# Two edge layers of a graph network: six steps for a group of edges in place of three, results of the matrix engine read one group later, more buffers for gathered rows, and a gate split into pieces

## The chip, the cores and the metric

The kernel runs on one core of one Trainium2 chip. A core has five engines that run side by side, each with its own queue of instructions: TensorE (PE in the profile; its weight loads have a row of their own, PEld), VectorE (DVE), ScalarE (ACT), GpSimd (POOL) and SyncE (SP), which issues most of the plain transfers. Engines wait for each other through semaphores. The metric is the device time of one execution in microseconds, the median over runs.

## The reference

There are 3125 nodes with 256 features each and 53125 edges, given in the order of their destination node. Four layers follow each other; each adds its result to `x` and starts from a layer norm of `x`.

```python
x = x + L0_gnn(layernorm(x), edge_index, edge_weight, ...)
x = x + L0_ffn(layernorm(x), ...)      # mixture of 16 experts, two for each node
x = x + L1_gnn(layernorm(x), ..., src, dst, edge_type)
x = x + L1_ffn(layernorm(x), ...)      # half of the nodes, chosen by a router
```

The first graph layer (layer 0) sums over the edges of a source node, with four heads:

```python
score = a_s[:, src] + a_d[:, dst] + aw_e * elem + ab
w = exp(-relu(score / 20.0))
out = segment_sum(w * feats[dst], src) / segment_sum(w, src)
```

The second (layer 1) sums over the edges of a destination node, with 200 types of relation:

```python
score = h[src] @ w_src + h[dst] @ w_dst + rel_emb[etype] @ w_rel
alpha = exp(leaky_relu(score)); alpha = alpha / alpha
agg = segment_sum((h[src] + rel_emb[etype]) @ weight_neighbor * alpha, dst)
x = x + relu(agg) + where(in_deg > 0, h @ loop_weight, h @ evolve_loop_weight)
```

The router of the last layer takes one weight for each node, `z @ wr + br`, and the 1561 nodes with the largest weights go through a feed-forward layer with weights `w1` (256 x 1024) and `w2` (1024 x 256).

## The kernel before

Edges are sorted by the block of 128 nodes that they are summed into. There are 25 blocks; each of the first 24 has room for 18 tiles of 128 edges, the last for 8. A tile is one edge for each of the 128 partitions. Six tiles make a group (`GRP`), so 24 blocks have three groups each and the last has one of six tiles and one of two: 74 groups and 440 tiles in a layer. Both graph layers run the same loop (`pipelined`, L966) over the stages that `edge_stages` (L874) returns, with their own `messages` and `finish`.

In a step of the loop each stage works on another group: `gather` on group g, `message` on g - 1, `add` on g - 2.

- `gather` fetches the far nodes' rows from a table in HBM, one indirect transfer by POOL for each tile (L907), into `rows`, of which there are `deep` buffers: five in layer 0, four in layer 1. It makes on DVE the one-hot `oh` of each edge's place in the block (L915), and from a transfer that repeats the edges' places over all partitions (`wide`, L897, on SP) the transposed masks `hot` (L924; three for a group in layer 1, one in layer 0).
- `message` multiplies the masks on TensorE with the near nodes' scores (L933), reads the sum from PSUM on DVE (`near`, L940), and calls `messages`. In layer 0 that is three small DVE steps, two exponentials on ACT and the scaling of the rows on DVE (L1099). In layer 1 it is an add (L1636), the weight with its exponential (L1595 to L1598), a one-hot of the relation written beside the row (L1639), and the one-hot `oh` scaled by each edge's weight on ACT into a second tile, `ohw` (L1645).
- `add` multiplies one-hots with rows on TensorE and sums a block in PSUM (L953). After a block's last group DVE reads the sum (`acc`, L961) and `finish` runs.

In layer 0, `finish` divides by the sum of weights and adds to `x`, and `done` of `gate` (L1185) runs for the tiles that are complete: after tiles 5, 10, 15, 20, 23 and 25 it normalizes them, turns them, multiplies them with the gate's weights (L1196), adds the bias (L1200), and after tiles 15, 23 and 25 picks the two experts (`choose`, L1148). In layer 1, `loops` (L1650, called as `early`) multiplies a block's nodes with both loop weights (L1654) into `held_ps`; `finish` (L1660) turns the counts of relations (L1666, L1669), multiplies them with the relations' features (L1672), and adds everything to `x` on DVE (L1679 to L1689).

PSUM is short: `ps_hold` holds constant numbers in its first half (`numbers`, read by L915 and L1639) and in its second half `held_ps` (the exponentials in layer 0, loop products in layer 1); `ps_sums` holds two blocks' sums; four buffers of one bank each (`ps_b`) serve all the rest.

After layer 1, `depths` (L1950) runs. `route` (L1732) normalizes the nodes in two batches (tiles 0 to 21, then 22 to 24) and takes their weights for the router on DVE (L1740), and stores them to HBM (ztab, L1746). The square root of its first batch (L167) has a dependency on the layer's last gather. `chosen` finds the 1561 largest, their rows are gathered (L1970), and the feed-forward layer follows (L2016, L2028). Its weights `w1` and `w2` are loaded by `router` (L1706, L1708), ahead of layer 1.

The order of each engine's instructions isn't that of the program. A planner lists them when the kernel is built: earlier lines of the program go first, but what is ready in the planner's own view of time may pass what is not. `keep_in_program_order` ties an instruction behind the one that the program wrote before it for the same engine.

Of the kernel before, what the change touches and what calls it, by code (L numbers as in the profile page):

```python
# [22 lines left out]
class _Kernel:  # L23
# [850 lines left out]
    def edge_stages(  # L874
        self, pool, st, table, width, into, near, others, messages, W, sums, finish, early=None, deep=3
    ):

# [24 lines left out]
        def gather(g, b, k, n, head, last):  # L902
            if head:
                now[b] = [spread(i, b) for i in range(len(st["wide"]))]
            rows = pool.tile([P, G, into], F32, name="rows", bufs=deep)
            for j in range(n):
                self.last_gather = nc.gpsimd.indirect_dma_start(  # L907
                    out=rows[:, j, :width], out_offset=None, in_=table,
                    in_offset=bass.IndirectOffsetOnAxis(
                        ap=st["idx"][:, k + j : k + j + 1], axis=0  # L910
                    ),
                )
            sh = [P, n, P]
            oh = pool.tile([P, G, P], F32, name="oh", bufs=3)
            nc.vector.tensor_tensor(  # L915
                oh[:, :n, :], numbers[:, None, :P].to_broadcast(sh),
                st["row"][:, k : k + n, None].to_broadcast(sh), op=OP.is_equal,
            )
            lo = (k - self.first[b]) // 2
            hots = []  # L920
            for i, (at, _) in enumerate([(self.pcol1, None)] + others):
                w = now[b][min(i, 1)][:, lo : lo + n // 2, : 2 * P]
                t = pool.tile([P, G // 2, 2 * P], BF16, name=f"hot{i}", bufs=2)
                nc.vector.tensor_scalar(t[:, : n // 2, :], w, at, None, op0=OP.is_equal)  # L924
                hots.append(t)
            return rows, oh, hots

        def message(g, b, k, n, head, last, rows, oh, hots):
            pe = self.ps_b("ps_near")
            picks = [near[:, b]] + [v for _, v in others]  # L930
            for j in range(n):
                for i, (t, v) in enumerate(zip(hots, picks)):
# [5 lines left out]
                    )  # L938
            own = pool.tile([P, G, nv], F32, name="near")
            nc.vector.tensor_reduce(  # L940
                own[:, :n, :],
                pe[:, : n * 3 * nv].rearrange("p (j q v) -> p j v q", q=3, v=nv), AX.X, OP.add,
            )
            if early is not None and k - self.first[b] == G:
                early(b)
            return messages(k, n, rows, own, oh)

        def add(g, b, k, n, head, last, oh, msg):
            if head:
                now["sum"] = sums2[:, b % 2 * 512 : (b % 2 + 1) * 512]  # L950
            ps = now["sum"]
            for j in range(n):
                nc.tensor.matmul(  # L953
                    ps[:, :W], oh[:, j, :], msg[:, j, :],
                    start=(head and j == 0), stop=(last and j == n - 1),
                )
            if last:
                more = pool.tile([P, W], F32, name="more")
                nc.sync.dma_start(more, sums[b])
                acc = pool.tile([P, W], F32, name="acc")  # L960
                nc.vector.tensor_add(acc, ps[:, :W], more)  # L961
                finish(b, acc)

        return gather, message, add

    def pipelined(self, stages, fill=()):  # L966
# [4 lines left out]
        for step in range(len(groups) + len(stages) - 1):  # L971
            if step > 2:
                next(fill, None)
            for i, stage in enumerate(stages):
                g = step - i
                if 0 <= g < len(groups):
                    done[g] = stage(g, *groups[g], *(done.pop(g, None) or ()))
# [77 lines left out]
    def heads_edges(self, st, fill, done):  # L1055
# [26 lines left out]
        with self.tc.tile_pool(name="edge0", bufs=2) as pool:  # L1082
# [7 lines left out]
            def messages(k, n, rows, near, oh):  # L1090
# [13 lines left out]
                return oh, rows  # L1104

            def finish(b, acc):
# [7 lines left out]
                done(b)  # L1114

            self.pipelined(self.edge_stages(
                pool, st, self.table0, W, W, near, [], messages, W, self.sums0, finish, deep=5
            ), fill)

    def gate(self, pool):


        nc, a, NT, D = self.nc, self.a, self.NT, self.D
# [59 lines left out]
        def done(b):  # L1185
            if b + 1 not in ends:
                return
            i = ends.index(b + 1)
            t0, t1 = ends[i - 1] if i else 0, b + 1
            self.norm_tiles(xn, t0, t1)  # L1190
            nc.sync.dma_start(xv[:, t0:t1, :], xn[:, t0:t1, :])
            pl = self.ps_b("ps_logit")
# [7 lines left out]
            nc.vector.tensor_tensor(  # L1200
# [3 lines left out]
            )  # L1204
            if t1 in choices:
                choose(choices[choices.index(t1) - 1], t1)

        return done
# [412 lines left out]
    def relations_edges(self, st):  # L1621
# [4 lines left out]
        with self.tc.tile_pool(name="edge1", bufs=2) as pool:  # L1626
# [7 lines left out]
            def messages(k, n, rows, near, oh):  # L1634
# [8 lines left out]
                ow = pool.tile([P, G, P], F32, name="ohw", bufs=3)  # L1643
                for j in range(n):
                    nc.scalar.activation(  # L1645
                        ow[:, j, :], oh[:, j, :], AF.Copy, scale=s[:, 1, j : j + 1]
                    )
                return ow, rows
# [11 lines left out]
            def finish(t, acc):  # L1660
# [10 lines left out]
                for i, (r0, n) in enumerate(rc):  # L1671
# [3 lines left out]
                    )  # L1675
                pw = self.held_ps
                xt = self.x[:, t, :]
                v = pool.tile([P, D], F32, name="agg")
                nc.vector.tensor_add(v, acc[:, :D], pr[:, :D])  # L1679
# [14 lines left out]
                early=loops, deep=4,  # L1694
# [4 lines left out]
    def router(self, pool):  # L1699
# [5 lines left out]
        w1 = pool.tile([P, C, HID], F32, name="w1")  # L1705
        nc.sync.dma_start(w1, a["L1_ffn_w1"].rearrange("(c p) h -> p c h", p=P))  # L1706
        w2 = pool.tile([P, HC, D], F32, name="w2")
        nc.sync.dma_start(w2, a["L1_ffn_w2"].rearrange("(c p) d -> p c d", p=P))  # L1708
# [12 lines left out]
        self.ffn_w = w1, w2, b1, b2  # L1721
# [228 lines left out]
    def depths(self):  # L1950
# [6 lines left out]
        w1, w2, b1, b2 = self.ffn_w  # L1957
        with self.tc.tile_pool(name="whom", bufs=1) as pool:
            for t in range(NT):
                self.route(t)  # L1960
# [197 lines left out]
```

## Time and profile before

| | |
|---|---|
| median of 10 runs | 2010.92 us (2007.0 to 2015.16) |
| the profiled execution | 2009.2 us, of which the span of its instructions is 2007.5 us |
| TensorE busy | 1470.6 us (73%) |
| VectorE busy | 1170.1 us (58%) |
| GpSimd busy | 1124.0 us (56%) |
| ScalarE busy | 423.8 us (21%) |
| gathers of layer 0 | first at 281.97 us, last ends at 836.10 us |
| gathers of layer 1 | first at 1287.37 us, last ends at 1841.57 us |
| weights of the router complete | 1872.6 us |
| first product of the feed-forward layer (L2016) | 1907.6 us |

Between the layers lie the experts (about 883 to 1230 us) and the features of layer 1. A line of the groups gives the source line, the engine, the operation, output<-inputs by the program's names, how often it ran, its busy time with the mean in nanoseconds, and then the idle time of the engine just before it with what ended most of that; "issue" is time in which the engine waited for nothing that the profile shows. A line of the waits gives who waited for whom, the total in microseconds, how many times, and the longest. A line of the timeline gives start, duration, engine and line, and in square brackets the idle time before it. In a table of windows a pair stands for each engine: busy time and, in brackets, instructions.

### The profile page before, as it was taken

The page shows a single profiled execution, that of the slowest core. Times are in us where ns is not written, and L with a number is a line of the kernel's source. Part 1 is how long each engine was busy: PE and PEld are TensorE (multiplying, and loading weights), DVE is VectorE, ACT ScalarE, POOL GpSimd, SP SyncE. Part 2 cuts the span into 40 slices and gives each one's busy share as a digit, 9 for nine tenths or more (in the row PEclk, how much of TensorE's full clock was granted, in tenths as well). Part 3 has the DMA queues.
Part 4 walks back from the last instruction along what each step waited for, and adds up shares of the span by engine and source line. Part 5 has one row for each costly group of instructions (what it writes and reads, how often), then busy time and mean ns, then how long its engine had stood idle before and what let it go on. Part 6 is the DMA issues. An engine that isn't in the chain of part 4 may idle for free. (4 is left out here: it accounts for less than half of the span.)

```text
span 2007.5 us, 22343 instructions
## 1 busy us (share of the span) xinstructions
PE 1470.6 (73%) x6602; PEld 920.6 (46%) x6602; DVE 1170.1 (58%) x3010; ACT 423.8 (21%) x1148; POOL 1124.0 (56%) x1133
## 2 busy tenths in 40 slices
PE   3677705475665666639999996498898888897398
PEld 1155504354444444426666664344444444443266
DVE  8999925575656665653322224467676677665631
ACT  1311100010101001102122223433233233334221
POOL 1058867777777777513333320267777777775051
PEclk8589957777777777759999998789999999998699
DMA  3042134454555555349899995575556655663140
GB/s 112 1 154 77 31 100 132 133 161 135 155 142 151 137 154 143 107 154 340 305 313 317 316 312 173 181 206 171 162 165 177 174 163 162 171 170 96 61 137 17
DMA packets 250714, 324.52 MB, mean 162 GB/s; under 512 B 38128, under 2 KB 185008, under 8 KB 250582
## 3 DMA queue, kind: packets, MB, share of 16 engines
q1 hardware_dynamic: 192214, 179.00, 28.4%
q0 software_dynamic: 51760, 137.35, 24.4%
q10 hardware_dynamic: 6608, 6.62, 1.0%
q8 instruction: 57, 0.93, 0.2%
q14 instruction: 75, 0.61, 0.1%
HBM read 286.26 MB, written 36.61 MB: 161 GB/s over the span
## 5 line engine op out<-in xcount | busy, mean ns | idle before, releaser
L907 POOL DMA_INDIRECT rows<-table,s_idx x880 | 835.6, 950 | 282.3 <-issue 236.1
L953 PE MATMUL ps_sums<-rows,oh 128*128 128x260 f32 x880 | 286.1, 493 | 163.1 <-issue 150.2
L953 PE MATMUL ps_sums<-rows,ohw 128*128 128x457 f32 x880 | 369.2, 561 | 10.1 <-ACT ohw L1645 9.9
L953 PEld LDWEIGHTS ps_sums<-rows,oh 128*128 128x128 f32 x880 | 214.3, 251 | 222.5 <-issue 162.7
L953 PEld LDWEIGHTS ps_sums<-rows,ohw 128*128 128x128 f32 x880 | 163.1, 194 | 167.9 <-issue 120.4
L1387 PE MATMUL ps_h<-w,x_t 128*128 128x512 f32 x448 | 203.9, 597 | 0.0
L924 DVE TENSOR_SCALAR hot<-wide,pcols 128x768 bf16<-128x768 bf16 (+1 forms) x296 | 174.1, 594 | 13.6 <-DMA wide<-s_w 7.5
L1409 POOL DMA_INDIRECT ytab<-y,back x56 | 55.0, 981 | 204.2 <-DVE y L1408 195.3
L1393 DVE TENSOR_TENSOR hid<-hid,ps_h 128x512 f32<-128x512 f32 x56 | 38.5, 688 | 198.7 <-ACT hid L1392 198.7
L915 DVE TENSOR_TENSOR oh<-ps_hold,s_row 128x768 f32<-128x768 f32 (+1 forms) x148 | 139.5, 942 | 20.8 <-PE ps_sums L953 20.8
L1645 ACT ACTIVATE ohw<-oh,s 128x128 f32<-128x128 f32 x440 | 136.4, 388 | 67.5 <-DVE s L1598 56.8
L609 POOL DMA_INDIRECT s_tab<-s_rec,s_to x65 | 124.5, 1916 | 30.4 <-issue 19.4
L1099 DVE TENSOR_TENSOR rows<-rows,ps_hold 128x1536 f32<-128x1536 f32 x74 | 128.3, 1733 | 0.6 <-ACT ps_hold L1097 0.3
L1387 PEld LDWEIGHTS ps_h<-w,x_t 128*128 128x128 f32 x448 | 81.5, 192 | 80.7 <-issue 80.6
L1093 DVE TENSOR_TENSOR s<-near,rows 128x24 f32<-128x24 f32 x74 | 13.6, 183 | 176.7 <-DMA rows<-table,s_idx 164.1
L1639 DVE TENSOR_TENSOR rows<-ps_hold,s_val 128x1200 f32<-128x1200 f32 x74 | 102.9, 1391 | 20.9 <-PE ps_hold L1654 20.8
L933 PEld LDWEIGHTS <-hot 128*128 128x128 bf16 x1760 | 61.6, 99 | 100.8 <-DVE hot L924 64.5
L1404 PE MATMUL ps_y<-w,h_t 128*128 128x256 f32 x448 | 105.9, 379 | 0.7 <-ACT h_t L202 0.7
L1097 ACT ACTIVATE ps_hold<-s 128x24 f32<-128x24 f32 x74 | 14.3, 193 | 434.5 <-DVE s L1095 235.8
L1404 PEld LDWEIGHTS ps_y<-w,h_t 128*128 128x128 f32 x448 | 85.0, 190 | 36.0 <-issue 26.3
L593 DVE TENSOR_TENSOR s_hv<-s_hk,s_dig 128x400 f16<-128x400 f16 x208 | 99.0, 648 | 0.0
L1362 POOL DMA_INDIRECT xg<-xtab,who x56 | 54.0, 964 | 77.5 <-DVE who_w L1337 46.3
(410 smaller groups left out, 2002.5 us busy)
## 6 DMA issues: line engine op xcount, KB each, us to landing
w<-in_L_ffn_w_dram SPq DMA_DIRECT2D x168, 512.0 KB
wide<-s_w SPq DMA_DIRECT2D x72, 576.0 KB
rows<-table,s_idx POOLq DMA_INDIRECT x880
sums<-sums_z SPq DMA_DIRECT2D x5, 1142.5 KB
more<-sums SPq DMA_DIRECT2D x25, 228.5 KB
yg<-ytab SPq DMA_DIRECT2D x5, 1024.0 KB
sums<-sums_z SPq DMA_DIRECT2D x5, 650.0 KB
table<-f ACTq DMA_DIRECT2D x5, 650.0 KB
```

The source lines that it names most:

```text
L593: nc.vector.tensor_tensor(rec[:, i], hk[:, i, :, None, :].to_broadcast(sh), dig[:, None, :, t0 + 2 * i : t0 + 2 * i + 2].to_broadcast(sh), ...
L609: d = nc.gpsimd.indirect_dma_start(out=tab, out_offset=bass.IndirectOffsetOnAxis(ap=to[:, i : i + 1], axis=0), in_=out[:, k * CH * V : (k ...
L907: self.last_gather = nc.gpsimd.indirect_dma_start(out=rows[:, j, :width], out_offset=None, in_=table, in_offset=bass.IndirectOffsetOnAxis( ...
L915: nc.vector.tensor_tensor(oh[:, :n, :], numbers[:, None, :P].to_broadcast(sh), st["row"][:, k : k + n, None].to_broadcast(sh), op=OP.is_equal,
L924: nc.vector.tensor_scalar(t[:, : n // 2, :], w, at, None, op0=OP.is_equal)
L933: nc.tensor.matmul(pe[:, j * 3 * nv : (j + 1) * 3 * nv], t[:, j // 2, j % 2 * P : (j % 2 + 1) * P], v.rearrange("p q v -> p (q v)"), start ...
L953: nc.tensor.matmul(ps[:, :W], oh[:, j, :], msg[:, j, :], start=(head and j == 0), stop=(last and j == n - 1),)
L1099: nc.vector.tensor_tensor(rows[:, :n, :HO].rearrange("p j (h o) -> p j h o", o=O), rows[:, :n, :HO].rearrange("p j (h o) -> p j h o", o=O) ...
L1387: nc.tensor.matmul(ph[:, i * HID : (i + 1) * HID], xt[:, c, :], w12[:, i, c, :], start=(c == 0), stop=(c == C - 1),)
L1404: nc.tensor.matmul(py[:, :D], ht[:, c, :], w3[:, c, :], start=(c == 0), stop=(c == HC - 1))
L1639: nc.vector.tensor_tensor(rows[:, :n, R0:], self.numbers[:, None, :R].to_broadcast(sh), st["val"][:, k : k + n, None].to_broadcast(sh), op ...
L1645: nc.scalar.activation(ow[:, j, :], oh[:, j, :], AF.Copy, scale=s[:, 1, j : j + 1])
```

## The change

The loop has six stages. `gather` keeps the transfers and the masks. `pick` has the products of masks and near scores, and makes `oh`, of which there are now four buffers. `message` reads `near` and calls `messages`. `add` has the products and issues the load of `more`. `finished` calls `early`, reads `acc` and calls `finish`. `closed` calls `close`, a new second part of layer 1's `finish` that begins with `agg`. A group so passes `message` two steps after its gather instead of one, `add` three steps after it instead of two, and its block is read one or two steps later again.

The DVE reads of `near`, `acc`, `agg` and `logits` are tied to program order. `rows` has seven buffers in layer 0 and six in layer 1. In layer 1 ACT scales `oh` in place, and the three buffers of `ohw` go. `done` of the gate is a generator: the norm and the store in one step, the turned tiles and products in the next, the bias and the choice in a third; its products go to the second half of `held_ps` and no longer to a buffer of `ps_b`. `w1` and `w2` are loaded in `depths`, in the pool that is opened after layer 1's.

```diff
-        def gather(g, b, k, n, head, last):
+        def gather(z, b, k, n, head, last):
...
-            sh = [P, n, P]
-            oh = pool.tile([P, G, P], F32, name="oh", bufs=3)
-            nc.vector.tensor_tensor(
-                oh[:, :n, :], numbers[:, None, :P].to_broadcast(sh),
-                st["row"][:, k : k + n, None].to_broadcast(sh), op=OP.is_equal,
-            )
...
-        def message(g, b, k, n, head, last, rows, oh, hots):
-            pe = self.ps_b("ps_near")
+        def pick(z, b, k, n, head, last):
+            z["pe"] = pe = self.ps_b("ps_near")
...
+            sh = [P, n, P]
+            z["oh"] = oh = pool.tile([P, G, P], F32, name="oh", bufs=4)
+            nc.vector.tensor_tensor(
+                oh[:, :n, :], numbers[:, None, :P].to_broadcast(sh),
+                st["row"][:, k : k + n, None].to_broadcast(sh), op=OP.is_equal,
+            )
+
+        def message(z, b, k, n, head, last):
             own = pool.tile([P, G, nv], F32, name="near")
-            nc.vector.tensor_reduce(
+            self.tc.keep_in_program_order(nc.vector.tensor_reduce(
                 own[:, :n, :],
-                pe[:, : n * 3 * nv].rearrange("p (j q v) -> p j v q", q=3, v=nv), AX.X, OP.add,
-            )
+                z["pe"][:, : n * 3 * nv].rearrange("p (j q v) -> p j v q", q=3, v=nv),
+                AX.X, OP.add,
+            ))
+            messages(k, n, z["rows"], own, z["oh"])
+
+        def add(z, b, k, n, head, last):
+            if head:
+                now["sum"] = sums2[:, b % 2 * 512 : (b % 2 + 1) * 512]
+            z["sum"] = ps = now["sum"]
+            for j in range(n):
+                nc.tensor.matmul(
+                    ps[:, :W], z["oh"][:, j, :], z["rows"][:, j, :],
+                    start=(head and j == 0), stop=(last and j == n - 1),
+                )
+            if last:
+                z["more"] = more = pool.tile([P, W], F32, name="more")
+                nc.sync.dma_start(more, sums[b])
+
+        def finished(z, b, k, n, head, last):
             if early is not None and k - self.first[b] == G:
                 early(b)
...
             if last:
-                more = pool.tile([P, W], F32, name="more")
-                nc.sync.dma_start(more, sums[b])
                 acc = pool.tile([P, W], F32, name="acc")
-                nc.vector.tensor_add(acc, ps[:, :W], more)
-                finish(b, acc)
-
-        return gather, message, add
+                self.tc.keep_in_program_order(
+                    nc.vector.tensor_add(acc, z["sum"][:, :W], z["more"])
+                )
+                z["done"] = finish(b, acc)
+
+        def closed(z, b, k, n, head, last):
+            if last and close is not None:
+                close(b, z["done"])
+
+        return gather, pick, message, add, finished, closed
...
+            for p in pending:
+                next(p, None)
...
-                done(b)
-
+                if b + 1 in done.ends:
+                    pending.append(done(b + 1))
+
+            pending = []
             self.pipelined(self.edge_stages(
-                pool, st, self.table0, W, W, near, [], messages, W, self.sums0, finish, deep=5
-            ), fill)
+                pool, st, self.table0, W, W, near, [], messages, W, self.sums0, finish, deep=7
+            ), fill, pending)
...
+            t0 = max([0] + [e for e in ends if e < t1])
             self.norm_tiles(xn, t0, t1)
             nc.sync.dma_start(xv[:, t0:t1, :], xn[:, t0:t1, :])
-            pl = self.ps_b("ps_logit")
+            yield
+            pl = self.held_ps[:, 256:512]
...
+            yield
+            tc.keep_in_program_order(nc.vector.tensor_tensor(
                 self.logits[:, t0:t1, :],
...
-                ow = pool.tile([P, G, P], F32, name="ohw", bufs=3)
                 for j in range(n):
                     nc.scalar.activation(
-                        ow[:, j, :], oh[:, j, :], AF.Copy, scale=s[:, 1, j : j + 1]
-                    )
-                return ow, rows
+                        oh[:, j, :], oh[:, j, :], AF.Copy, scale=s[:, 1, j : j + 1]
+                    )
...
+                return acc, pr
+
+            def close(t, sums):
+                acc, pr = sums
                 pw = self.held_ps
                 xt = self.x[:, t, :]
                 v = pool.tile([P, D], F32, name="agg")
-                nc.vector.tensor_add(v, acc[:, :D], pr[:, :D])
+                self.tc.keep_in_program_order(nc.vector.tensor_add(v, acc[:, :D], pr[:, :D]))
...
-                early=loops, deep=4,
+                close=close, early=loops, deep=6,
...
-        w1 = pool.tile([P, C, HID], F32, name="w1")
-        nc.sync.dma_start(w1, a["L1_ffn_w1"].rearrange("(c p) h -> p c h", p=P))
-        w2 = pool.tile([P, HC, D], F32, name="w2")
-        nc.sync.dma_start(w2, a["L1_ffn_w2"].rearrange("(c p) d -> p c d", p=P))
...
         with self.tc.tile_pool(name="whom", bufs=1) as pool:
+            w1 = pool.tile([P, C, HID], F32, name="w1")
+            nc.sync.dma_start(w1, a["L1_ffn_w1"].rearrange("(c p) h -> p c h", p=P))
+            w2 = pool.tile([P, HC, D], F32, name="w2")
+            nc.sync.dma_start(w2, a["L1_ffn_w2"].rearrange("(c p) d -> p c d", p=P))
```

## The prediction

> **What bounds the kernel now.** I read the groups by line first, then the gathers' own line, the waits of GpSimd (POOL), a table of windows, and the timelines around the places where an edge layer starts and stops. Numbered from 0, a layer has 74 groups (72 of six and, in the last block, one of six and one of two), so 440 gathers.
>
> ```profile
> L907 POOL DMA_INDIRECT rows<-table,s_idx x880 | 835.6, 950 | 282.3 <-issue 236.1
> ```
>
> ```profile
> POOL rows L907 <- issue: 236.1, 773, 1.2
> POOL rows L907 <- PE ps_sums L953: 15.5, 38, 4.2
> ```
>
> The gathers are 950 ns each, and of 282.3 us of idle time before them 236.1 us is "issue": 773 pauses of 0.305 us in which nothing was waited for. So a gather takes a slot of 1.25 us and a group 7.5 us. Layer 0's gathers run from 281.97 to 836.10 us, layer 1's from 1287.37 to 1841.57 us: 554.1 and 554.2 us for 440 slots, 551 by the slot. What is not slot is three microseconds per layer.
>
> ```profile
> core 0: us, PE busy (x) PEld busy (x) DVE busy (x) ACT busy (x) POOL busy (x), PEclk, DMA share, GB/s
> 282.00:838.00 556.00, 322.98 (x1441) 249.77 (x1442) 332.79 (x788) 53.80 (x185) 420.64 (x445) 0.75 0.53 145
> 1287.00:1843.40 556.40, 473.00 (x2449) 236.39 (x2449) 370.99 (x949) 168.65 (x568) 416.53 (x440) 0.94 0.62 173
> 1843.40:1873.00 29.60, 18.88 (x52) 8.88 (x52) 18.51 (x91) 21.29 (x51) 0.00 (x0) 0.79 0.32 107
> ```
>
> VectorE (DVE) has 333 and 371 us of work in 556, at most 5.0 us of a group's 7.5; TensorE (PE) 473, 6.4 us. Neither is full. So inside a layer POOL sets the pace, and the other engines matter where POOL waits for them, and after its last gather. The one long wait is near layer 1's start:
>
> ```profile
> 1321.38 0.94 POOL L907 DMA_INDIRECT rows<-table,s_idx  x1 [4.24 <-PE ps_sums L953]
> ```
>
> Group 4 wants the buffer of group 0, whose product was late. The other place is the end of layer 1:
>
> ```profile
> 1829.78 1.86 ACT L1645 ACTIVATE ohw<-oh,s 128x128 f32<-128x128 f32 x6 [0.98 <-DVE s L1598]
> 1831.66 1.28 ACT L167 ACT_TABLE_LOAD   x1
> 1843.40 0.31 ACT L167 ACTIVATE ln_rs<-mv,eps 128x22 f32<-128x22 f32 x1 [10.46 <-DMA rows<-table,s_idx]
> 1843.73 1.28 ACT L1596 ACT_TABLE_LOAD   x1
> 1845.03 0.30 ACT L1596 ACTIVATE s<-s 128x6 f32<-128x6 f32 x2
> ```
>
> ScalarE (ACT) scales group 70, then stands 10.46 us at a square root that is tied to the last gather; the exponentials of 71 and 72, in its queue behind it, follow at 1845.03. From the landing (1843.4) to the router's last weights (1872.6) pass 29.2 us, and nothing of the next stage can start before.
>
> **The change, part by part.** The profiled execution took 2009.2 us (span 2007.5, 1.7 around it); the median shown is 2010.92, 1.7 above. I add changes to the median.
>
> *Rows of seven and six groups.* In layer 1 the pause of 4.24 us becomes a common one of 0.30: **-3.94 us**. Group 6 will want group 0's buffer, at 1287.37 + 6 x 7.5 = 1332.4, 11 us after 1321.4. In layer 0 no gather lost time to a buffer: measured from the gather that reuses it, a group's products ended at least 4.7 us earlier. Its two pauses over 0.35 us are short POOL jobs for the next stage (0.45, 0.81, 0.15, 0.17 and 0.21 us). Fuller memory may push them behind the layer, where POOL is idle: 0 to -1.8 us; I take 0, as nothing shows their place gone.
>
> The Trainium skill, Perfetto Trace Analysis (Optimization Strategy), reads a gap that repeats on the engine that should be full as a possible lack of room for the next tile. By that rule the 236 us of pauses might go. The rows say "issue" for 773 of them and name a buffer for one long one, so the sum keeps 3.94.
>
> *TensorE's results read later.* The reads are `near`, `acc`, `agg` and `logits`. In layer 1 DVE waited 55.8 us for `agg` (23 times) and 33.9 us for `acc`; in layer 0 13.4 us for `near`. Almost all of that goes, and is costed at nothing: POOL's slots cover it (7.5 us against 5.0 of DVE work). If that cover failed it would be worth up to 90 us in layer 1. Behind a read that is pinned stand, in DVE's queue, the hot masks and one-hots of later groups; who waits for them is TensorE, with two to four groups of rows in hand. A group's products now come one step later (7.5 us), and the buffers give two groups more (15 us), so the room before a gather stalls grows by 7.5 us, to about 12 in layer 0 and 14 in layer 1 (median 6.6 there).
>
> *In-place scaling, `oh` in `pick`.* As many instructions as before: 440 activations of 388 ns, 148 one-hots of 942 ns. Nothing.
>
> *w1 and w2 loaded late.* SP issued them at 1285.96 and 1286.86 us, 0.99 us together; the next loads move up, which lets group 0 start earlier and is already in the 3.94. They now wait until the layer's memory is free, at latest 1868.3 (last read of its tiles). The nearest row for their length is the stretch 1285.96 to 1298.2 in which they and layer 1's loop weights came: 12.3 us at most, so 1881, 26 us before the first use (L2016, 1907.6). On SP's queue they stand near the eight ztab stores (1850.8 to 1871.9), wanted at 1901.3: 29 us of cover. Nothing; without cover, up to 12.3.
>
> *Gate in pieces.* Norm, logits and choice of five tiles are spread over three steps, and the logits go into `ps_hold`, which ACT and DVE use for every group. The wait for such sharing shows in layer 1: DVE's L1639 waited 20.8 us in 24 times for L1654, 0.87 each, though it reads the other half of the tile. In mid-layer the rows in hand cover it. At layer 0's end it can sit between the last groups: at most the 3.4 us from the first logits product to the last of tiles 20 to 22 (822.56 to 825.94). The choice of tiles 15 to 22, begun at 826.5, starts later; it has DVE's 4.0 idle us before the last logits (853.42). For a gain: 4.0 us, if the last groups, whose rows were scaled 4 us after landing (841.9), flow freely. Bounds -4.0 and +3.4; the nearest row for either is the present end, so 0.
>
> The Trainium skill, PSUM (section on bank collisions), asks for a guard by bank and quadrant. `numbers` and `held_ps` lie in different banks, so by that rule the one-hots would not wait for logits and this part would end at -4.0 to 0. The 20.8 us show that here the wait is by tile.
>
> *The end of layer 1.* The planner that writes each engine's order takes the square root as soon as it believes the last gather landed; in its view gathers run ahead as far as buffers allow. Before, group 73 takes group 69's buffer, and the root stands behind group 70, which is in the same step as 69's products. Now group 73 takes 67's, and the message of that step is 68. The root also wants tile 21's statistics, which come with the new last step, behind 68's rows and beside 69's. So the root moves ahead of group 70, one group earlier than now (two, if ahead of 69). What it holds back has to be done after the landing. One group's work there is 6 x 0.385 = 2.3 us of TensorE at the least (weight loads 0.385 apart) and 5.0 us of DVE at the most (371/74); DVE has 18.5 of the 29.6 us filled. Between: **+3.65 us**. Bounds: two groups, +7.3 to +10; below, a tail free of its waits for TensorE (acc 2.5, agg 2.0, ct 4.6 in these 29 us) is 9.1 shorter.
>
> Sum: -3.94 + 3.65 = -0.3; 2010.92 - 0.3 = **2010.6 us**.
>
> **Rivals.** *Both ends drain faster.* The reads that made DVE and ACT wait in the tails come later, the root stays where it is, and layer 0 gives its 4.0: -3.94 - 4.0 - 9.1/2 = -12.5, so 1998.4 us. For it: those 9.1 us are there. Against: the root has stood where buffers let it.
>
> *The root moves by two groups* (ends slower). Place: ACT's queue ahead of group 69's exponential; DVE's reciprocals behind it stand as well. Price: +7.3 to +10 less 3.94, and layer 0's +3.4 possibly: +3.4 to +9.5, middle +6.5, 2017.4 us. It decides from +8 in the tail on. For it: the buffer count alone says two. Against: the statistics of tile 21 come late.
>
> *The step becomes longer than POOL's slot.* Four PSUM buffers now hold two `near` and one `rel` at a time; if TensorE (6.4 of 7.5 us) has to wait 1.4 us a group, layer 1 paces by it. 0.3 us a group over 74 is +22, 2033 us. The lag of products gives no sign.
>
> *The change does nothing inside the layers* is not a rival but part of all four but the last.
>
> **How the numbers follow.** Chances: the forecast 0.38, faster ends 0.27, root by two groups 0.29, longer step 0.06. About 0.2% (4.0 us) is what a measurement of this kernel tells from no change. The forecast's own range is 2005 to 2015; of its 0.38, 0.34 lie within 0.2%, 0.01 faster, 0.03 slower. Of the faster ends 0.25 are over 0.2% faster, 0.02 within. Of the root's 0.29, 0.27 slower, 0.02 within. Faster 0.26, same 0.38, slower 0.36. The range leaves out the longer step and a tenth at the faster end: 1999 to 2022.
>
> **What would show it.** Right: gathers 1.25 us apart to the end in both layers, no pause over 1 us in layer 1, its stretch 550.3 us; DVE's waits for `agg`, `acc` and `near` gone; ACT's square root ahead of group 70's exponential with a wait over 15 us; landing to last router weight near 33 us. Wrong: DVE's waits for `agg` still there; a root behind group 71; gathers that wait for `ps_sums`; a first L2016 that waits for w1; a layer 0 end (landing to logits of the last tiles, now 838 to 853.4) that differs by over 4 us.

## The result and the profile after

The changed kernel took 2027.17 us (median of 8 runs) against 2010.92: a ratio of 1.0081, 95% interval 1.0072 to 1.009. It is 16.3 us slower, where -0.3 us was forecast. The profiled execution took 2026.48 us (span 2024.4).

Set against the profile before, stage by stage (us, from the gathers' and the later stages' first and last instructions). The landing, at which the last gather's rows have arrived, comes 1.8 us after that gather's own end (1841.57 and 1843.40 before):

| stretch | before | after | difference |
|---|---|---|---|
| layer 0, first to last gather | 554.13 | 554.06 | -0.1 |
| layer 0's end, last gather to first fetch of the experts | 46.26 | 51.78 | **+5.5** |
| from there to layer 1's first gather | 405.01 | 403.72 | -1.3 |
| layer 1, first to last gather | 554.20 | 550.24 | **-4.0** |
| layer 1's end, last gather to the last router weight | 31.02 | 48.18 | **+17.2** |
| from there to the end | 134.87 | 134.69 | -0.2 |

With -0.2 us ahead of layer 0 this is the 17.0 us between the two spans. The -1.3 is within what this stretch does by itself: it lay between 403.4 and 408.3 us in the other runs below, which leave the experts alone.

The gathers kept their slot and layer 1 lost its pause. The groups by line, and then the waits of GpSimd, of the changed kernel:

```profile
L910 POOL DMA_INDIRECT rows<-table,s_idx x880 | 836.9, 951 | 279.0 <-issue 232.4
```

```profile
POOL rows L910 <- issue: 232.4, 763, 0.3
POOL rows L910 <- PE ps_sums L956: 14.6, 48, 0.3
```

The longest pause is 0.3 us; before, one for `ps_sums` was 4.24. So the inside of the layers went as forecast. The two ends did not. ScalarE's timeline at the end of layer 1 (start, duration, engine and line, operation, and in brackets the idle time before it with what ended it):

```profile
1813.19 1.28 ACT L1664 ACTIVATE oh<-oh,s 128x128 f32<-128x128 f32 x4
1843.44 1.28 ACT L167 ACT_TABLE_LOAD   x1 [28.98 <-DMA rows<-table,s_idx]
1844.74 0.32 ACT L167 ACTIVATE ln_rs<-mv,eps 128x22 f32<-128x22 f32 x1
1845.07 1.28 ACT L1616 ACT_TABLE_LOAD   x1
1846.37 0.21 ACT L1616 ACTIVATE s<-s 128x6 f32<-128x6 f32 x1
1846.48 0.35 ACT L202 COPY x_t<-ps_x_t 128x256 f32<-128x256 f32 x1
```

The scaling that ends at 1814.5 is group 68's; the exponential at 1846.37 is group 69's. Between them ScalarE stood 28.98 us at the square root (L167), waiting for the last gather, and before it was 10.46. This time the table load waited too, so its 1.28 us come after the landing. What that stop did to TensorE, in the same window:

```profile
1822.39 0.19 PE L929 MATMUL ps_near<-rel_p,hot 128*128 128x3 bf16 x2
1846.89 3.78 PE L1672 MATMUL ps_hold<-lw,x_t 128*128 128x512 f32 x4 [24.31 <-ACT x_t L202]
1850.46 5.08 PE L956 MATMUL ps_sums<-rows,oh 128*128 128x457 f32 x12
```

TensorE's next instruction was a loop product whose `x_t` ScalarE copies; that copy stood behind the root. For 24.31 us TensorE did nothing, though the rows of groups 69 and 70 had landed by 1826 (their scaling stood behind the root too). VectorE stood as well, at the reciprocal that takes the root's result and that has all later work of its queue behind it; before, this wait was 2.59 us:

```profile
1845.09 0.29 DVE L176 RECIPROCAL ln_rs<-ln_rs 128x22 f32<-128x22 f32 x1 [23.40 <-ACT ln_rs L167]
```

One more thing is to be read in the last line of TensorE's timeline: the products of one group of six tiles are 12 records and took 5.08 us (4.86 for group 68's from 1817.08 on, where the granted clock was 1.00). And busy time by engine from the landing to the last weight (the columns are PE, PEld, DVE, ACT, POOL, then the granted clock, the DMA share and GB/s):

```profile
1843.40:1890.00 46.60, 33.62 (x110) 16.06 (x110) 29.01 (x121) 27.98 (x70) 0.00 (x0) 0.87 0.26 86
```

Before, this stretch was 29.6 us with 18.88 us of TensorE and 18.51 us of VectorE in it. Behind the landing TensorE's busy time grew by 14.7 us and VectorE's by 10.5, and the end by 17.2.

At layer 0's end, VectorE's timeline:

```profile
838.06 0.42 DVE L937 TENSOR_TENSOR oh<-ps_hold,s_row 128x256 f32<-128x256 f32 x1 [5.21 <-PE ps_hold L1214]
...
841.28 0.20 DVE L1219 TENSOR_TENSOR logits<-ps_hold,gb 128x48 f32<-128x48 f32 x1
841.52 0.29 DVE L1177 TENSOR_REDUCE tmp_c<-logits 128x8 f32<-128x128 f32 x1
...
846.94 0.18 DVE L944 TENSOR_REDUCE near<-ps_near 128x8 f32<-128x24 f32 x1
...
848.27 0.69 DVE L1118 TENSOR_TENSOR rows<-rows,ps_hold 128x512 f32<-128x512 f32 x1 [0.31 <-ACT ps_hold L1116]
...
859.26 0.19 DVE L1219 TENSOR_TENSOR logits<-ps_hold,gb 128x32 f32<-128x32 f32 x1 [2.87 <-PE ps_hold L1214]
```

VectorE first stands 5.21 us at the last group's one-hot, which waits for the gate's products (L1214) in the other half of `ps_hold`. The choice of tiles 15 to 22 (L1177 on) begins at 841.5, after the last gather, and the last group's `near` stands behind nearly all of it. That group's rows are scaled at 848.27 (841.90 before), and the last logits follow at 859.26 (853.42 before).

### The profile page after: what moved, and what is told of

Its sections match the earlier page's. It is cut to its first block, busy times and chain, and to the rows that moved or that the text cites. A ratio compares the mean times of both kernels' runs of the same rounds, so it can differ in the third digit from the quotient of the medians.

```text
span 2024.4 us, 22251 instructions
## 1 busy us (share of the span) xinstructions
PE 1492.9 (74%) x6602; PEld 952.2 (47%) x6602; DVE 1189.0 (59%) x3010; ACT 417.3 (21%) x1148; POOL 1126.3 (56%) x1133
## 3 DMA queue, kind: packets, MB, share of 16 engines
q0 software_dynamic: 51760, 137.35, 24.4%
## 5 line engine op out<-in xcount | busy, mean ns | idle before, releaser
L956 PE MATMUL ps_sums<-rows,oh 128*128 128x260 f32 (+1 forms) x1760 | 688.7, 546 | 195.5 <-issue 180.9
L956 PEld LDWEIGHTS ps_sums<-rows,oh 128*128 128x128 f32 x1760 | 390.8, 231 | 399.3 <-issue 322.8
L921 DVE TENSOR_SCALAR hot<-wide,pcols 128x768 bf16<-128x768 bf16 (+1 forms) x296 | 171.2, 598 | 44.8 <-PE ps_near L929 27.6
L1664 ACT ACTIVATE oh<-oh,s 128x128 f32<-128x128 f32 x440 | 137.8, 389 | 60.0 <-DVE s L1618 59.0
L1112 DVE TENSOR_TENSOR s<-near,rows 128x24 f32<-128x24 f32 x74 | 13.6, 184 | 159.1 <-DMA rows<-table,s_idx 144.9
L929 PEld LDWEIGHTS <-hot 128*128 128x128 bf16 x1760 | 69.1, 98 | 61.0 <-issue 29.1
L593 DVE TENSOR_TENSOR s_hv<-s_hk,s_dig 128x400 f16<-128x400 f16 x208 | 91.1, 494 | 0.0
L598 PE MATMUL s_mv<-s_hv,s_hp 128*128 128x200 f16 x416 | 68.6, 268 | 24.6 <-DVE s_hv L593 18.5
L200 PE MATMUL ps_x_t<-ident,xn 128*128 128x128 f32 x200 | 47.0, 324 | 50.6 <-DVE xn L190 29.6
```

The source lines that it names most:

```text
L593: nc.vector.tensor_tensor(rec[:, i], hk[:, i, :, None, :].to_broadcast(sh), dig[:, None, :, t0 + 2 * i : t0 + 2 * i + 2].to_broadcast(sh), ...
L929: nc.tensor.matmul(pe[:, j * 3 * nv : (j + 1) * 3 * nv], t[:, j // 2, j % 2 * P : (j % 2 + 1) * P], v.rearrange("p q v -> p (q v)"), start ...
L956: nc.tensor.matmul(ps[:, :W], z["oh"][:, j, :], z["rows"][:, j, :], start=(head and j == 0), stop=(last and j == n - 1),)
L1664: nc.scalar.activation(oh[:, j, :], oh[:, j, :], AF.Copy, scale=s[:, 1, j : j + 1])
```

## The experiments

Two theories for layer 1's end were set against each other. R: the number of `rows` buffers decides where the square root stands in ScalarE's queue, and that place makes the end. S: the six steps by themselves make it, because loops, `acc` and `agg` now come later in the order of the program. All "ends" below are measured as in the table above.

**Fewer buffers, all else of the change (e1).**

```diff
-                pool, st, self.table0, W, W, near, [], messages, W, self.sums0, finish, deep=7
+                pool, st, self.table0, W, W, near, [], messages, W, self.sums0, finish, deep=5
...
-                close=close, early=loops, deep=6,
+                close=close, early=loops, deep=4,
```

> The changed kernel with rows of five and four groups again; six steps, pinned reads, gate in pieces and late w1 and w2 stay. Two theories of the 17.1 us by which layer 1's end (last gather's landing to the last router weight) grew from 29.2 to 46.4 us. R, the square root: the number of rows buffers decides where the root stands in ScalarE's queue, and with six it stands ahead of group 69's exponential. S, the six steps: loops, `acc` and `agg` now come later in the order of the program, wherever the root stands. R expects the root behind group 71's exponential, an end of 25 to 33 us, and 2006 to 2014 us in all (layer 0's end keeps its 5.5). S expects an end over 40 us and 2021 to 2029. Layer 1's pause near its start: the first product would leave 15.2 - 15 = 0.2 us of room, so at most 1 us of pause by either.

Measured: 2010.46 us, ratio 0.9999 (0.999 to 1.0008); layer 1's end 31.3 us. ScalarE's timeline:

```profile
1837.84 0.21 ACT L1616 ACTIVATE s<-s 128x6 f32<-128x6 f32 x1 [1.05 <-DVE s L1615]
1838.06 1.28 ACT L167 ACT_TABLE_LOAD   x1
1846.46 0.31 ACT L167 ACTIVATE ln_rs<-mv,eps 128x22 f32<-128x22 f32 x1 [7.12 <-DMA rows<-table,s_idx]
```

The root now stands behind group 71's exponential and waits 7.12 us. R holds: two numbers in the source, which leave the six steps alone, take back the 17 us. A pause of 1.24 us at the layer's start (1 us expected at most) is the price.

**The root last (e2).**

```diff
+            self.scales = []
...
-                    nc.scalar.activation(
+                    last = nc.scalar.activation(
                         oh[:, j, :], oh[:, j, :], AF.Copy, scale=s[:, 1, j : j + 1]
                     )
+                self.scales.append(last)
...
-            self.norm_tiles(z, t0, t1, self.mv2, self.last_gather, scalar=True)
+            self.norm_tiles(z, t0, t1, self.mv2, self.scales[73], scalar=True)
```

> The changed kernel with one dependency altered: the first square root waits for the last group's last scaling on ScalarE in place of the last gather. R expects that groups 69 to 73 are scaled as their rows land, so the end shrinks from 46.4 to between 22 and 30 us (PE and DVE had 18.9 and 18.5 us of work in the 29.6 us of before), 2003 to 2011 us in all. S expects little: over 40 us and 2021 to 2029.

Measured: 2008.05 us, ratio 0.999 (0.9982 to 0.9999); the end 28.0 us. With six steps and all buffers in place, one dependency gives back 20 us of the end. S falls as the account of the 17 us.

**The gate in one step (e3).**

```diff
-            yield
             pl = self.held_ps[:, 256:512]
...
-            yield
+            if False:
+                yield
             tc.keep_in_program_order(nc.vector.tensor_tensor(
```

> The changed kernel with the gate's pieces run in one step (no pauses between norm, logits and choice); the logits stay in ps_hold and their read stays pinned. If the pieces put the choice of tiles 15 to 22 in front of the last rows, layer 0's end (last gather to first fetch, 46.3 before, 51.8 after) returns to 46 to 48 and the whole is 2021 to 2024 us. If the later `finished` step alone does it (accumulators read one step later, so tile 22 is ready a group later), it stays at 51 to 52 and 2027.

Measured: 2023.26 us, ratio 1.0064 (1.005 to 1.0077); layer 0's end 44.8 us. The choice starts at 830.7 there, ahead of the last landing, and the last group's rows are scaled at 839.35. In this kernel the last group's one-hot runs at 834.02 and waits for nothing. So the pieces cost 7.0 us, and the rest of the change gains 1.5 at this end (46.3 before).

**Three steps with six buffers (e4).** The kernel before, `deep=6` in layer 1, `w1` and `w2` loaded as in the change, `oh` scaled in place with four buffers.

```diff
-                early=loops, deep=4,
+                early=loops, deep=6,
```

> The kernel before with six rows buffers in layer 1 (five in layer 0 as before), w1 and w2 loaded late and the one-hots scaled in place, which makes the room: three steps, no pins, gate whole. R expects the root one group earlier than before, ahead of group 70, and an end longer than 29.2: by the prediction's price, 3.65, it is 33 us and with the pause of 3.94 gone 2010 to 2011 us in all; by half of what two groups cost in the changed kernel, 8.5, it is 38 us and 2014 to 2017. S expects an end of 29 us and 2006 to 2008.

Measured: 2018.47 us, ratio 1.0043 (1.0029 to 1.0057); the end 44.6 us. Without any of the six steps the end is 13.6 us longer than before. The root again, and what TensorE waited for:

```profile
1816.43 1.28 ACT L167 ACT_TABLE_LOAD   x1
1837.48 0.31 ACT L167 ACTIVATE ln_rs<-mv,eps 128x22 f32<-128x22 f32 x1 [19.77 <-DMA rows<-table,s_idx]
1837.70 0.25 ACT L1668 COPY ct<-ps_cnt 128x128 f32<-128x128 f32 x1
```

```profile
1838.00 0.43 PE L1665 MATMUL ps_cnt<-ident,acc 128*72 128x128 f32 x1 [21.77 <-ACT ct L1668]
```

Here a small copy of counts (`ct`, 0.25 us) stands behind the root and stops TensorE for 21.77 us, in the middle of group 69's products. VectorE stood 22.76 us at its reciprocal. The root moved by one group, the move that the prediction priced at 3.65, but its price was 13.6. The expectation's larger value, 8.5, was too small as well.

**Both repairs (f1)**: the root last and the gate in one step, on the changed kernel.

> The changed kernel with both repairs: square root behind the last scaling, gate in one step. If the two losses are separate, the end of layer 0 is that of the run with the whole gate (44.8 us from the last gather to the first fetch) and the end of layer 1 that of the run with the root last (28.0 us from the last gather to the last router weight, 31.0 before): 2008.05 less 3.9 to 6.6, so 2001 to 2005. If they share a cause, no better than 2008.

Measured: 2001.82 us, ratio 0.9962 (0.995 to 0.9974), ends 45.1 and 29.3 us. The two losses are separate, and without them the change gains 9 us on the kernel before.

**And the loops early (f2)**, which the prediction had not priced: the change also moves `early` from the step of the messages to `finished`.

```diff
+            if early is not None and k - self.first[b] == G:
+                early(b)
             messages(k, n, z["rows"], own, z["oh"])
...
-            if early is not None and k - self.first[b] == G:
-                early(b)
             if last:
                 acc = pool.tile([P, W], F32, name="acc")
```

> The same with the loop products at their old place, in the step that makes a group's messages, three steps earlier than the change puts them. If the moved loops share in the longer end (with the root last, TensorE still waits 1.35 us for a loop's x_t and makes three loop products of 2.0 us after the landing), the end of layer 1 falls by 2 to 6 us below 28.0. If TensorE has the room, it stays at 27 to 28 and the whole is the same as without.

Measured: 2005.15 us, ratio 0.9969 (0.9957 to 0.998), the end 29.9 us (29.3 in f1, which took 3.3 us less in all). `message` is two stages ahead of `finished`, and not three as the expectation says. In this kernel a block's closing step reads the loop products after those of the next block have taken their place, so that part of the sum is another block's; the instructions are the same in number and kind. Moving the loops back gains nothing at the end, so with the root last their later place is not a cause of its own. In the changed kernel a loop product was the instruction at which TensorE was caught.

**Three steps, six buffers, the root last (f3).** The edit of e4 with that of e2.

> The kernel before with six rows buffers in layer 1, one-hots scaled in place, w1 and w2 late and the square root behind the last scaling: no six steps, no pins, gate whole. By R the end of layer 1 falls from the 44.6 us of six rows and three steps to 24 to 30, with no pause at its start: 1999 to 2005 us. If six steps and pinned reads are worth something by themselves, the changed kernel with both repairs is faster than this one by over 2 us; if not, they are within 2 us of each other.

Measured: 1998.38 us, ratio 0.9942 (0.9929 to 0.9955), the end 24.3 us. The end is 5.0 us shorter than that of the changed kernel with both repairs (29.3), and layer 0's end 1.8 longer (46.9 against 45.1). Together the two ends make 3.2 us; the medians differ by 3.4 and the profiled spans by 1.5, since f1's profiled execution began layer 0 1.5 us sooner. So the six steps are not what makes the repaired kernel fast: they lengthen layer 1's end, with the last two blocks' `acc` done 12.8 and 20.0 us after the last gather, against 1.1 and 12.3 in three steps. The pins are not the reason: without them (f4, next) that end is no shorter.

**No pins (f4).** The kernel with both repairs, without the four `keep_in_program_order` around `near`, `acc`, `agg` and `logits`.

> The changed kernel with both repairs and without its four pinned reads (near, acc, agg, logits): the planner may place them as it likes. The prediction put the pinned reads at 0 inside the layers: the layers' stretches stay at 550 to 555 us each, the gathers show no pause over 2 us, and the whole is within 2 us of the kernel with both repairs. If the pins carry the gathers, pauses for ps_sums come back and it is slower by over 4 us.

Measured: 2009.68 us, ratio 0.9995 (0.9986 to 1.0003), 7.9 us slower than with pins. VectorE's waits in layer 1:

```profile
DVE agg L1702 <- PE ps_rel L1691: 68.5, 23, 4.0
```

The wait for `agg` is back and larger than the 55.8 us of the kernel before, and yet the gathers show no pause over 0.3 us and the layer's stretch is 550.6 us. The prediction's "nothing inside the layers" holds. The 7.9 us (8.9 between the profiled spans) come from elsewhere: layer 0's end is 50.3 us against 45.1, where the planner, left free, reads the logits of tiles 20 to 22 at 834.7 and not at 829.8, layer 1's end is 0.7 longer, and 2.3 us stand in the stretch of the experts, which no pin touches.

**The price of the root's place in the kernel before.** Six runs for this (g1 to g3, then h1 to h3) fell into two series of runs in which the kernel before itself took 2329 and 2300 us, with gathers that waited for products throughout both layers, so their times stand only against their own kernel before. There the late weights alone (g3) showed no difference beyond the interval:

> The kernel before with w1 and w2 loaded late and nothing else. The prediction put this at nothing: first hidden product behind the choice, not behind w1, and the end of layer 1 and all after it as before: 2009.5 to 2012.5 us. If the loads collide with the ztab stores or come late, 2013 to 2023; if layer 1 starts sooner without them, group 0's gathers come up to 2 us sooner and it is 2008 to 2010.

Measured: ratio 1.0012 (0.9979 to 1.0046), the end 29.2 us. The five others there:

| kernel | ratio (95% interval) | layer 1's end, us |
|---|---|---|
| g1, root last alone | 1.0027 (1.0003 to 1.005) | 31.0 |
| h1, the same | 1.003 (0.9992 to 1.0067) | 31.0 |
| h2, rows of five and late weights | 0.9996 (0.9965 to 1.0028) | 37.6 |
| g2, six buffers, root in three parts | 1.0032 (1.0005 to 1.0059) | 40.6 |
| h3, the same | 1.0051 (1.0023 to 1.008) | 40.6 |

So in these two series, where gathers waited for products, neither a root put last nor one in three parts gained anything, and the last of these kernels had the longest end. Why was not examined; what follows holds for the series at 2011 us. The three kernels were run again in one in which the kernel before took 2011.13 us (on the chip numbered 2; the first eight experiments ran on number 3). First the kernel before with the root last, its only edit (k1):

> The kernel before, rows of five and four, with the square root behind the last scaling and nothing else. On the chip of the first eight experiments: if the root held back groups 71 and 72 in the kernel before too, the end of layer 1 falls from 31.0 us to 24 to 27, 2003 to 2007 us in all; if a root behind group 70 was free, 31 and 2010 to 2011.

Measured: 2005.27 us, ratio 0.9971 (0.9962 to 0.9981), the end 24.3 us, with the pause of 4.4 us still at the layer's start. So the root cost 6.7 us where it already stood.

One buffer more and the late weights, nothing else (k2):

```diff
-                early=loops, deep=4,
+                early=loops, deep=5,
```

> The kernel before with five rows buffers in layer 1 in place of four and w1 and w2 late. The root stands ahead of group 70's exponential, behind the counts of the block before. By the prediction's price of one group the end is 34.7 us (31.0 + 3.65) and the whole 2010 to 2011; by 4.85 us of products for each group held back and the chain to them, 38 to 45 us and 2014 to 2021.

Measured: 2013.57 us, ratio 1.0013 (1.0003 to 1.0023), the end 36.8 us, no pause. One buffer moves the root ahead of group 70's exponential, takes back the pause and leaves the kernel 2.4 us slower than the one before.

Last, a kernel (k3) that takes work out of the end: three steps, six buffers, the root of tiles 0 to 16 in the middle of the layer, of 17 to 21 behind the last scaling.

```diff
-        ends = [NT - 3, NT]
+        ends = [NT - 8, NT - 3, NT]
...
-            self.norm_tiles(z, t0, t1, self.mv2, self.last_gather, scalar=True)
+            self.norm_tiles(z, t0, t1, self.mv2, self.scales[73] if t0 else self.scales[53], scalar=True)
```

> Three steps, six rows buffers, w1 and w2 late, scaling in place, and the root of 25 tiles in three parts: tiles 0 to 16 behind group 53's scaling, 17 to 21 behind the last scaling, 22 to 24 at the end. If ScalarE and VectorE bound the end once the root is last, it falls from 24.3 us to between 18 and 22 and the whole to 1992 to 1997; if the chain of products, counts and sums bounds it, it stays at 23 to 24 and 1996 to 1999.

Measured: 1995.39 us, ratio 0.9927 (0.9907 to 0.9946), the end 19.9 us, no pause over 0.3. Windows from the landing to the last weight, of f3, from which only the root's parts differ, and then of k3 (columns as above):

```profile
1839.60:1862.10 22.50, 11.03 (x39) 5.15 (x37) 16.36 (x83) 17.04 (x39) 0.00 (x0) 0.82 0.46 148
```

```profile
1839.60:1858.00 18.40, 10.97 (x39) 5.14 (x37) 11.23 (x50) 8.85 (x22) 0.00 (x0) 0.85 0.24 81
```

TensorE has the same 11.0 us in both; ScalarE falls from 17.04 to 8.85, VectorE from 16.36 to 11.23, and the end by 4.4. So once the root is last, ScalarE's and VectorE's share of the normalisations makes at least these 4.4 us of the end; which of the two engines does was not separated. Beside the kernel before it is faster, and by its median also than f3 (1998.38), though the intervals of these two ratios overlap.

The ends of the series at 2011 us together. Busy times are those between landing and last weight, read from the same view:

| kernel | where the root stands | layer 1's end, us | TensorE busy in it, us | VectorE busy in it, us |
|---|---|---|---|---|
| k3, three steps | last, five tiles | 19.9 | 11.0 | 11.2 |
| k1 and f3, three steps | last | 24.3 | 11.0 | 16.4 |
| e2, six steps | last | 28.0 | 13.6 | 18.3 |
| f1, six steps, gate whole | last | 29.3 | 14.6 | 18.3 |
| f4, as f1 without pins | last | 30.0 | 21.4 | 21.2 |
| before, three steps | behind group 70 | 31.0 | 18.9 | 18.5 |
| e1, six steps | behind 71's exponential | 31.3 | 19.8 | 21.4 |
| k2, three steps | ahead of group 70, behind the counts | 36.8 | 26.5 | 24.4 |
| e4, three steps | ahead of group 70 and of the counts | 44.6 | 33.0 | 29.0 |
| after, six steps | ahead of group 69 | 48.2 | 33.6 | 29.0 |

## Why the prediction was wrong

**Rows of seven and six.** Right. The pause went, -3.96 us against -3.94 forecast, and layer 0's stretch did not move.

**TensorE's results read later.** Right inside the layers: `acc` waits 0.3 us in place of 33.9, `near` nothing. The sign "DVE's waits for `agg` gone" was half wrong, and something came in its place. VectorE's waits in layer 1 of the changed kernel:

```profile
DVE oh L937 <- PE ps_hold L1672: 57.0, 22, 7.1
DVE s L1656 <- DMA rows<-table,s_idx: 37.0, 21, 4.2
DVE agg L1701 <- PE ps_rel L1690: 27.4, 14, 3.4
```

The one-hots now wait for the loop products, though they read the other half of `ps_hold`. That is the wait by tile which the prediction set against the Trainium skill's PSUM page (title "PSUM — Partial Sum Buffer", section on bank collisions), which asks for a guard by bank and quadrant: in this program the wait goes further than that guard asks, as the row said, and the 57.0 us of it cost the layer's stretch nothing (550.24 us). What the prediction did not price is the pins' worth at the ends, in f4 5.1 us at layer 0's.

**w1 and w2 late.** Right. SP issued them at 1886.06 and 1886.48 us, later than the 1868.3 reckoned, yet the first hidden product came 6.3 us after the first fetch, as before.

**Gate in pieces.** Wrong: 0 taken, bounds -4.0 and +3.4, measured +5.5, and 7.0 by e3. The step that failed is "it has DVE's 4.0 idle us before the last logits (853.42)". The choice was not put into that idle time, but into VectorE's queue ahead of the last group's `near`, where it delays the chain that ends in those logits. The bound was taken from the length of the logits' products, 3.4 us, and was too small: the wait for the shared tile alone was 5.21 us at the last one-hot, and the choice stood from 841.5 to 846.9 ahead of the last rows. In e3, with neither at that place, group 72's rows are scaled 3.4 us sooner (836.16, not 839.61) and the last group's 8.9 (839.35, not 848.27). How much of the 7.0 us is the wait's and how much the choice's was not separated.

**The end of layer 1.** Wrong twice. The place: "one group earlier than now (two, if ahead of 69)". It was ahead of 69, because tile 21's statistics come in the step in which 68's messages are made and not one later. The rival with two groups named this place. The price is the larger error: "6 x 0.385 = 2.3 us of TensorE at the least", "Between: +3.65 us", and for two groups +7.3 to +10; measured 5.8 and 13.6 for one (k2, e4) and 17.2 for two. A group of six tiles has 12 weight loads and 12 matmuls, two of each for a tile, and takes 4.85 us. The prediction counted six. Its own row of 473 us of TensorE in 74 groups, 6.4 each, would have shown it. And it priced one group's work where the queue matters: a root that stands stops every later instruction of ScalarE, among them 0.25 to 0.35 us copies (`ct`, `x_t`) that TensorE's queue waits for in order, and VectorE's reciprocal with all that is behind it. So TensorE stood for 16.3 us (k2), 21.8 (e4) and 24.3 (after), VectorE for 14.1, 22.8 and 23.4, and their work came behind the landing. In the table above the end grows with that pushed work: against the kernel before, +7.6 us of TensorE came with +5.8, +14.1 with +13.6, +14.7 with +17.2, and VectorE's busy time grew by 5.9, 10.5 and 10.5. No run separates the two engines, and busy time alone is no price: f4, in which no root stops them, has 6.8 us more of TensorE than f1 and an end only 0.7 longer. The 2.5 us by which the last end exceeds TensorE's growth were not split; the table load after the landing (1.28) may be in them. The loop product at half clock (3.78 us in place of 1.88) is in the 14.7.

The moved loops were not priced at all; f2 shows that, with the root last, their place gains or costs nothing at the end that can be told apart (29.9 against 29.3).

The sum by the terms: -4.0 at layer 1's start, +5.5 in place of 0, +17.2 in place of +3.65, -1.7 in the rest. The forecast's range ended at 2022, below the 2027.2 measured, since its upper end was built on the small price.

## What to carry to other kernels

A tuning number can decide more than room: here the count of `rows` buffers moved a waiting square root in ScalarE's queue (e1, k2, e4). That it does so by telling the planner how early the last gather may land fits these places; the planner's own times were not read. When a wait is moved ahead in an in-order queue, price all work of all engines that it pushes behind the event, by their busy time after it, and not the one group that it passes; here TensorE's growth came within 2.5 us of the end's in three kernels that a root stopped, and it is an index and not the cost, as f4 shows. And tie an instruction that must come late to the last instruction that it may hold up, not to a transfer whose time the planner has to guess; that gained 5.9 to 20 us where POOL's slots set the pace (k1, e4 to f3, after to e2), and nothing where the gathers waited for products (g1, h1).

## What the runs showed of the hardware

After 24.3 us without work TensorE's first four matmul records of a loop product took 3.78 us, where the same four took 1.88 at 1870.2; after 9.6 us in the kernel before, 12 records of products took 7.40 us in place of 4.85. The granted clock (third number from the end) in the first part of each, in the kernel before and then in the changed one:

```profile
1846.17:1851.20 5.03, 5.03 (x7) 2.48 (x8) 1.35 (x8) 5.03 (x16) 0.00 (x0) 0.50 0.02 3
```

```profile
1846.89:1850.46 3.57, 3.57 (x4) 1.51 (x5) 0.54 (x3) 3.57 (x10) 0.00 (x0) 0.50 0.00 0
```

From 1817.10 to 1821.90 of the changed kernel, in the midst of work, it was 1.00. The Trainium skill's page "TensorE: Matmul & The Clock Gate" (Part 1) says that an array left idle for some 3.4 us falls to half rate until it has been busy as long. The rows agree in the halving; the half rate lasted 5.0 us and 3.6 us or more here.

In two series of runs the same unchanged kernel took 2329 and 2300 us, against 2011 in the others. They ran on the chips numbered 0 and 2, and k1 to k3 found 2011 us on number 2, so whether it was the chip or the time is open. In one profile of the first series (g3) the gathers waited 194.3 us for `ps_sums` in 35 waits of up to 17.0 us, against 15.5 us in 38 before, while a gather still took 0.95 us; the mean granted clock was 0.793 there and 0.851 before. Why its products came later was not examined.
